# Two layers of graph attention: layer 1's sums in two PSUM banks, its denominators by a matmul of their own, and the second tile's first blocks at the layer change

## The chip, the cores and the metric

The kernel runs on one core of a Trainium2 chip. The metric is the device time of one execution in microseconds (us). The engines are TensorE (PE, with its weight loads as PEld), VectorE (DVE), ScalarE (ACT), GpSimd (POOL), which here mainly issues gathers, and SyncE (SP), which issues the plain DMAs.

## The reference, cut to what matters

There are 3327 nodes with 1024 features, and an adjacency matrix in which about 17 entries of a row are set. Two layers follow each other; each is a graph attention, added to its input and layer-normed.

```python
def layer1(x, adj, W, a1, a2):                      # layer 0 is alike, with 8 heads of 128
    h = x @ W
    e = leaky_relu(h @ a1 + (h @ a2).T, 0.2)
    attention = softmax(where(adj > 0, e, -9e15), axis=1)
    return relu(attention @ h)

x = layernorm(x + layer0(x, adj, ...))
x = layernorm(x + layer1(x, adj, ...))
```

## The kernel before, in words

Nodes are taken in 26 tiles of 128 rows (`NT`). The first part of the kernel makes layer 0's `h` and, for every tile of target rows, lists of the sources that its rows need. The second part, `sparse`, uses these lists. It runs a list of 52 items in order: 26 of class `Layer0` and 26 of class `Target` (layer 1). The prediction calls the latter T0 to T25.

An item works in five blocks of sources, b0 to b4. (Some tiles of layer 0 have two of these done earlier.) For b0 to b3, POOL issues four indirect gathers (`gather`, L1032) of 128 rows each into one of five buffers (`NS`; the profile shows two as `near` and three as `src`). Block b4 (`EB`) is one gather into one of two buffers `end`. The gathers go out in the order of the list `fetches`; `send` issues the next one when a buffer is free and, for layer 1, when the rows of `y_d` that it may read are stored. For b0 and b1 the first half of the tiles must be stored, for b2 to b4 all of them. Five of the early blocks of T0, T1 and T2 stand ahead in that list (`ahead_of`).

In layer 1 a block then takes two steps. In `weights`, DVE makes a 128x128 tile of weights in three operations: two write into columns 256 to 383 of `way`, a PSUM tile of one bank (L1222, L1223), the third writes `es` in SBUF (L1225). In `sums`, PE multiplies these by the gathered rows (L1234). A row of `y_d` holds 1024 values, a one for the denominator, and two factors of the weights. The 1025 columns are cut in three (`CUTS`), one PSUM bank each. In b0 to b3 the four groups of 32 targets use 32 columns of PE each.

When a tile's five blocks are summed, `close` adds the tile's own node, divides, and writes `z` (ACT and DVE). `finish` is a generator of ten steps: two sets of four transposes of `z`, then the projection by layer 1's `W` (`wt1`, L1266) in eight pairs of k-tiles, which PE does between the sums of the next tiles. After each half, DVE adds the residual (L1269). `settle` makes the layer norm and stores the rows.

`pipeline` writes the order of work out by hand. Every engine takes its instructions in that program order. For block j of item i it issues the `weights` of the next block, then the `sums` of this one, then `send` and `rest`, which runs the `finish` steps of the items before by the tables in `plans`. `prepare` of the next item, which loads its row of factors (`rr`), makes its marks (L1048, L1052) and loads its tile of `y_d`, is issued in the middle of an item's blocks. `own` makes a tile's own weight from that tile of `y_d`.

The layer change is at the last `Layer0` item. Its `finish` makes the norm (Sqrt on ACT) and two dot products on DVE, takes two Exp on ACT, and stores the tile's row into `y_d` (L1166). In `pipeline`, `turn` marks T0: four of these steps come ahead of its first weights.

PSUM has eight banks: six of tag A for sums and projections, one for transposes, one for `way`.

Of the kernel before, what the change touches and what calls it, by code (L numbers as in the profile page):

```python
# [19 lines left out]
P = 128  # L20
# [6 lines left out]
def kernel(  # L27
# [50 lines left out]
    HW0 = DW + 2 * H  # L78
    HW = D + 4
    HP = 1088  # L80
# [891 lines left out]
    def sparse(own):  # L972
# [9 lines left out]

        ys = [pool.tile([P, HW], F32, bufs=1, name=f"y{n}") for n in range(3)]
        for y in ys:
            nc.vector.memset(y[:, D:], 0.0)
            nc.vector.memset(y[:, D : D + 1], 1.0)

# [67 lines left out]
        class Layer0:  # L1055
# [86 lines left out]
            def finish(self):  # L1142

                ri = sbuf("ri", [P, H], 2)
                for n, acc in enumerate(self.acc):
                    nc.vector.reciprocal(ri[:, HEADS[n] : HEADS[n + 1]], acc[:, :, DH])
                t, row = self.t, self.y
                y = row[:, :D]
                for h in range(H):
                    yh = y[:, h * DH : (h + 1) * DH]  # L1150
                    nc.vector.scalar_tensor_tensor(  # L1151
                        yh, self.acc[h // 3][:, h % 3, :DH], ri[:, h : h + 1], yh, op0=OP.mult, op1=OP.add
                    )
                yield
                yield from ph.norm_steps([y])
                for n in range(2):
                    pr = sbuf("pr", [P, D], 1)
                    nc.vector.scalar_tensor_tensor(
                        pr, y, 1.0, wa[n], op0=OP.mult, op1=OP.mult, accum_out=r1.sd[:, t, n, :]
                    )  # L1160
                    if n == 0:
                        yield
                nc.scalar.activation(row[:, D + 1 : D + 2], r1.d[:, t, :], AF.Exp)
                nc.scalar.activation(row[:, D + 2 : D + 3], r1.d[:, t, :], AF.Exp, scale=SLOPE)
                nc.scalar.activation(grow[:, t : t + 1], r1.s[:, t, :], AF.Exp, scale=1 - SLOPE)
                nc.sync.dma_start(y_d[t * P : (t + 1) * P, :HW], row)  # L1166
                stored.add(t)
                yield
                tr = bank("T", [P, 4, P], "tr")
                nc.tensor.transpose(tr[:, 0, :], grow[:, t : t + 1].to_broadcast([P, P]), ident)  # L1170
                line = sbuf("line", [1, P], 2)
                nc.scalar.activation(line, tr[:1, 0, :], AF.Copy)
                nc.sync.dma_start(row_d[t], line)

        class Target:
# [3 lines left out]
            def __init__(self, t, n):  # L1179
                self.t, self.n, self.src, self.made, self.buf = t, n, {}, {}, {}  # L1180

# [15 lines left out]
            def own(self):  # L1197

                t, res = self.t, self.res
                es = self.es = sbuf("es1", [P, 2], 2)  # L1200
                nc.vector.scalar_tensor_tensor(
                    es[:, 1:], res[:, D + 1 : D + 2], grow[:, t : t + 1], res[:, D + 2 : D + 3], op0=OP.mult, op1=OP.max
                )
                nc.vector.tensor_tensor(es[:, :1], es[:, 1:], loop[:, t : t + 1], OP.mult)
# [7 lines left out]
            def begin(self):  # L1212
                self.acc = {c: bank("A", [P, CUTS[1]], "acc1") for c in (2, 0, 1)}

            def weights(self, b):
# [5 lines left out]
                oh = self.oh[:, b * NG : (b + 1) * NG, :] if b < EB else self.oh2.unsqueeze(1)  # L1221
                nc.vector.tensor_tensor(raw, r, s[:, :, D + 1 : D + 2].to_broadcast(wide), OP.mult)  # L1222
                nc.vector.tensor_tensor(raw, raw, s[:, :, D + 2 : D + 3].to_broadcast(wide), OP.max)  # L1223
                es = sbuf("es", [P, P], 3).rearrange("p (g t) -> p g t", g=ng)
                nc.vector.tensor_tensor(es, raw, oh, OP.mult)  # L1225
                self.made[b] = es

            def sums(self, b):
                es, s = self.made.pop(b), self.src.pop(b)
                for c in (2, 0, 1):  # L1230
                    m = CUTS[c + 1] - CUTS[c]
                    for g in range(NG if b < EB else 1):
                        to = slice(g * GT, (g + 1) * GT) if b < EB else slice(0, P)
                        nc.tensor.matmul(  # L1234
                            self.acc[c][to, :m], es[:, g, :], s[:, g, CUTS[c] : CUTS[c + 1]],
                            start=b == 0, stop=b == EB,
                        )

            def close(self):

                ri = sbuf("ri", [P, H], 2)
                nc.vector.tensor_tensor(ri[:, 2:3], self.acc[2][:, D - CUTS[2] : D - CUTS[2] + 1], self.es[:, :1], OP.add)
                nc.vector.reciprocal(ri[:, :1], ri[:, 2:3])
                nc.vector.tensor_tensor(ri[:, 1:2], ri[:, :1], self.es[:, :1], OP.mult)  # L1244
                z = self.z = sbuf("z", [P, D], 3)
                for c in (2, 0, 1):
                    cut = slice(CUTS[c], min(CUTS[c + 1], D))
                    nc.scalar.activation(z[:, cut], self.res[:, cut], AF.Copy, scale=ri[:, 1:2])  # L1248
                for c in (2, 0, 1):
                    cut = slice(CUTS[c], min(CUTS[c + 1], D))  # L1250
                    nc.vector.scalar_tensor_tensor(
                        z[:, cut], self.acc[c][:, : cut.stop - cut.start], ri[:, :1], z[:, cut],
                        op0=OP.mult, op1=OP.add,
                    )
# [43 lines left out]
        def pipeline(items, fetches):  # L1298
# [4 lines left out]
                len(Target.blocks) - HB: ((), (2, 1), (1, 1), (1,)),  # L1303
                Target: ((2,), (2, 1), (2, 1), (1, 1), (1, 1), (1,)),
            }

            def rest(i, n):
                it = items[i] if i < len(items) else items[-1]
                plan = plans[Target] if isinstance(it, Target) else plans[len(it.blocks)]
                for who in plan[n]:  # L1310
# [4 lines left out]
            def send():  # L1315
                while sent[0] < len(fetches):
# [3 lines left out]
                    items[i].fetch(b)  # L1320
                    sent[0] += 1

            def get(i):
# [11 lines left out]
            for i, it in enumerate(items):  # L1335
# [4 lines left out]
                for j, b in enumerate(it.blocks):  # L1340
# [8 lines left out]
                    if j == 0:  # L1349
                        get(i + 1)  # L1350
                    if j == nb // 2 and after:
                        after.prepare()
                    if j == 0:
                        it.own()
                    if j + 1 < nb:
                        it.weights(it.blocks[j + 1])
                    elif after and type(after) is type(it):
                        after.weights(after.blocks[0])
                    if j == 0:
                        it.scale_own()  # L1360
                    it.sums(b)
                    free[b == EB].append(it.buf.pop(b))
                    send()
# [18 lines left out]
        fetches = [(i, b) for i, it in enumerate(items[:NT]) for b in it.blocks][HB:]  # L1382
        ahead_of = [(NT + i, b) for i in range(3) for b in range(HB)][: NS]
        fetches += ahead_of
# [161 lines left out]
```

## Time and profile before

| | us |
|---|---|
| median of 3 runs | 1749.48 (1748.37 to 1754.7) |
| the profiled execution | 1751.44 |
| its span, first to last instruction | 1749.6 |
| up to the last layer 0 sums | 1069.8 |
| layer change, until PE runs on without a gap | about 50 |
| layer 1 in steady order, until T25's sums | 598.8 |
| the rest: T24's and T25's projection, last norm, store | 30.8 |

| engine | busy us of the span | share |
|---|---|---|
| PE | 1497.3 | 86% |
| DVE | 1143.2 | 65% |
| POOL | 1050.7 | 60% |
| ACT | 494.6 | 28% |

Each row of a profile's timeline has the start in us, the busy time in us, the engine, the source line (L1234), the operation, what it writes and reads by the program's names, shape and count. In brackets follow the engine's idle time just before it, and what ended that. PE's rows give modelled ends, so rates are read from start to start. PEclk or "granted clock" is TensorE's clock as a share of its full speed.

### The profile page before, as it was taken

The page shows a single profiled execution, that of the slowest core. Times are in us where ns is not written, and L with a number is a line of the kernel's source. Part 1 is how long each engine was busy: PE and PEld are TensorE (multiplying, and loading weights), DVE is VectorE, ACT ScalarE, POOL GpSimd, SP SyncE. Part 2 cuts the span into 40 slices and gives each one's busy share as a digit, 9 for nine tenths or more (in the row PEclk, how much of TensorE's full clock was granted, in tenths as well). Part 3 has the DMA queues.
Part 4 walks back from the last instruction along what each step waited for, and adds up shares of the span by engine and source line. Part 5 has one row for each costly group of instructions (what it writes and reads, how often), then busy time and mean ns, then how long its engine had stood idle before and what let it go on. Part 6 is the DMA issues. An engine that isn't in the chain of part 4 may idle for free.

```text
span 1749.6 us, 34204 instructions
## 1 busy us (share of the span) xinstructions
PE 1497.3 (86%) x12755; PEld 865.2 (49%) x12755; DVE 1143.2 (65%) x3126; ACT 494.6 (28%) x1424; POOL 1050.7 (60%) x1309
## 2 busy tenths in 40 slices
PE   9799989898998477676676664799999999999998
PEld 5566655565665355555555542344444444444443
DVE  6799998888886788676877765344444453444443
ACT  5677752232323133332332322011111011111110
POOL 5433155776775666555656666677667766676750
PEclk9999999999999699887888886899999999999999
DMA  7688988999999999999999999999999999999980
GB/s 186 123 157 164 185 232 305 316 388 348 360 346 355 371 410 412 398 396 384 396 396 386 390 384 383 359 401 393 396 399 386 394 392 387 388 394 410 386 336 36
DMA packets 190321, 596.13 MB, mean 341 GB/s; under 512 B 37914, under 2 KB 47924, under 8 KB 190146
## 3 DMA queue, kind: packets, MB, share of 16 engines
q0 software_dynamic: 131056, 459.23, 73.4%
q1 hardware_dynamic: 58932, 134.36, 20.5%
q8 instruction: 103, 1.69, 0.4%
q14 instruction: 72, 0.59, 0.1%
q10 hardware_dynamic: 158, 0.26, 0.0%
HBM read 593.70 MB, written 54.99 MB: 371 GB/s over the span
## 4 chain that ended last, share of the span: by engine, by line
PE 41%; DMA 17%; DVE 5%; issue 2%; POOL 1%; ACT 0%; DVEq 0%; SPq 0%; ACTq 0%; POOLq 0%
PE mm L1266 22%; PE acc L1234 13%; DMA src<-h_d,idx 7%; DMA own<-h_d 4%; PE acc L1134 3%; DMA near<-h_d,idx 2%; PE acc L1121 2%; DMA src<-y_d,idx 2%; DVE e L1108 2%; PE tr L203 1%; DVE pr L998 1%; DVE y L1151 1%; DMA end<-h_d,idx 1%; DMA av<-in_L_gnn_a_dram 1%; DMA half<-half_d 0%
## 5 line engine op out<-in xcount | busy, mean ns | idle before, releaser
L571 PE MATMUL mm<-wt,xT 128*128 128x384 f32 (+1 forms) x1248 | 415.3, 478 | 0.4 <-DMA xT<-in_x_t_dram 0.4
L1266 PE MATMUL mm<-wt,xT 128*128 128x512 f32 x832 | 387.6, 604 | 0.0
L1032 POOL DMA_INDIRECT src<-y_d,idx x248 | 251.4, 1014 | 122.6 <-PE acc L1234 48.2
L571 PEld LDWEIGHTS mm<-wt,xT 128*128 128x128 f32 x1248 | 230.7, 195 | 130.2 <-issue 36.0
L1266 PEld LDWEIGHTS mm<-wt,xT 128*128 128x128 f32 x832 | 149.7, 189 | 198.9 <-issue 194.0
L1269 DVE SCALAR_TENSOR_TENSOR o<-mm,y 128x512 f32<-128x512 f32 x52 | 35.9, 691 | 317.3 <-PE mm L1266 317.3
L1032 POOL DMA_INDIRECT src<-h_d,idx x152 | 160.2, 1054 | 108.3 <-PE acc L1134 24.8
L1032 POOL DMA_INDIRECT near<-y_d,idx x168 | 171.1, 1018 | 65.7 <-issue 21.7
L1134 PE MATMUL acc<-src,e 128*32 128x129 f32 x2432 | 103.4, 340 | 74.6 <-DVE e L1108 74.6
L691 POOL DMA_INDIRECT near<-h_d,idx x112 | 124.1, 1108 | 51.5 <-issue 23.9
L1032 POOL DMA_INDIRECT near<-h_d,idx x96 | 103.3, 1076 | 75.5 <-DMA src<-h_d,idx 28.6
L1234 PE MATMUL acc<-src,es 128*32 128x341 f32 x1488 | 124.8, 470 | 26.0 <-DVE es L1225 26.0
L1134 PEld LDWEIGHTS acc<-src,e 128*32 128x32 f32 x2432 | 86.8, 138 | 92.6 <-DVE e L1108 81.2
L1248 ACT ACTIVATE z<-y,ri 128x342 f32<-128x342 f32 (+1 forms) x78 | 39.5, 569 | 299.1 <-DVE ri L1244 299.1
L1134 PE MATMUL acc<-near,e 128*32 128x129 f32 x1664 | 68.8, 332 | 58.6 <-DVE e L1108 44.2
L1108 DVE TENSOR_TENSOR e<-oh,way 128x1024 f32<-128x1024 f32 x90 | 109.9, 1221 | 7.9 <-PE acc L1134 0.6
L206 ACT ACTIVATE xT<-tr 128x512 f32<-128x512 f32 x52 | 31.0, 597 | 236.0 <-PE tr L203 236.0
L1134 PEld LDWEIGHTS acc<-near,e 128*32 128x32 f32 x1664 | 57.8, 134 | 70.7 <-DVE e L1108 48.6
L1234 PEld LDWEIGHTS acc<-src,es 128*32 128x32 f32 x1488 | 43.1, 112 | 96.3 <-issue 43.9
L1121 PE MATMUL acc<-own,ident 128*128 128x387 f32 (+1 forms) x156 | 72.0, 547 | 16.7 <-ACT own L1090 16.7
L411 ACT ACTIVATE junk<-ad 128x1664 uint8<-128x1664 uint8 x52 | 83.0, 1595 | 7.6 <-POOL ad L400 6.1
L1234 PE MATMUL acc<-near,es 128*32 128x342 f32 (+1 forms) x1008 | 82.0, 458 | 1.5 <-DVE es L1225 1.5
(225 smaller groups left out, 2378.7 us busy)
## 6 DMA issues: line engine op xcount, KB each, us to landing
own<-h_d SPq DMA_DIRECT2D x26, 524.0 KB
y_d<-y SPq DMA_DIRECT2D x26, 514.0 KB
y<-y_d SPq DMA_DIRECT2D x26, 514.0 KB
xT<-in_x_t_dram SPq DMA_DIRECT2D x26, 512.0 KB
h_d<-ht SPq DMA_DIRECT2D x25, 524.0 KB
y<-in_x_dram SPq DMA_DIRECT2D x25, 512.0 KB
out_dram<-o SPq DMA_DIRECT2D x25, 512.0 KB
ad<-in_adj_dram POOLq DMA_DIRECT2D x25, 415.9 KB
```

The costliest lines, as they stand in the source:

```text
L206: nc.scalar.activation(part, tr, AF.Copy)
L411: nc.scalar.activation(junk, ad[:, n * THR : (n + 1) * THR], AF.Copy, accum_out=self.d[:, n : n + 1])
L571: nc.tensor.matmul(accs[t, c], xT[t][:, k, :], wt[:, k, CUTS0[c] : CUTS0[c + 1]], start=k == 0, stop=k == KT - 1)
L691: nc.gpsimd.indirect_dma_start(out=src[n % 3][:, g, :], out_offset=None, in_=h0_d[:THR, :], in_offset=bass.IndirectOffsetOnAxis(ap=idx[:, ...
L1032: nc.gpsimd.indirect_dma_start(out=s[:, g, :w], out_offset=None, in_=table[:n, :], in_offset=bass.IndirectOffsetOnAxis(ap=idx[:, t, b * NG ...
L1108: nc.vector.tensor_tensor(e, oh.unsqueeze(2).to_broadcast([P, ng, H, wide]), wp.unsqueeze(3).to_broadcast([P, ng, H, wide]), OP.mult,)
L1121: nc.tensor.matmul(self.acc[n].rearrange("p h d -> p (h d)"), ident, part, start=False, stop=False)
L1134: nc.tensor.matmul(self.acc[h // 3][g * GT : (g + 1) * GT, h % 3, :], e[:, g, h, :], rowsof[:, g, h, :], start=j == 0 and h in HEADS, stop ...
L1234: nc.tensor.matmul(self.acc[c][to, :m], es[:, g, :], s[:, g, CUTS[c] : CUTS[c + 1]], start=b == 0, stop=b == EB,)
L1248: nc.scalar.activation(z[:, cut], self.res[:, cut], AF.Copy, scale=ri[:, 1:2])
L1266: nc.tensor.matmul(acc, xT[:, k, :], wt1[:, k, half], start=k == 0, stop=k == KT - 1)
L1269: nc.vector.scalar_tensor_tensor(o[:, half], acc, 0.0, res[:, half], op0=OP.max, op1=OP.add)
```

## The change

It has four parts.

1. A row of `y_d` loses the one for the denominator (and an unused column): 1026 columns for 1028. Layer 1's sums go to two banks of 512 columns.
2. DVE adds up the tile's five weight tiles (`total`, four additions of 128x128). After the end block, PE multiplies `total` by a column of ones. The result is the denominator; it goes to column 384 or 385 of `way`. `close` reads it from there and works in halves.
3. At the layer change, after T0's b0 and b1, the new function `sums_ahead` prepares T1, makes its own weight, and issues the weights and sums of its b0 and b1; T1 has three blocks left then, with a plan of its own (`HB`). All six early blocks of T0 to T2 stand ahead in `fetches`, where there were five.
4. Ahead of the last `Layer0` tile's finish, ACT takes a Sqrt of ones that nothing uses (`warm`).

```diff
-    HW = D + 4
+    HW = D + 2
...
-        for y in ys:
-            nc.vector.memset(y[:, D:], 0.0)
-            nc.vector.memset(y[:, D : D + 1], 1.0)
+        ones = pool.tile([P, 1], F32, bufs=1, name="ones")
+        nc.vector.memset(ones, 1.0)
+        warm = pool.tile([P, 1], F32, bufs=1, name="warm")
...
             def finish(self):            # class Layer0
+                if self.n == NT - 1:
+                    nc.scalar.activation(warm, ones, AF.Sqrt)
...
             def own(self):               # class Target
                 t, res = self.t, self.res
+                if self.begun:
+                    return
...
             def begin(self):
-                self.acc = {c: bank("A", [P, CUTS[1]], "acc1") for c in (2, 0, 1)}
+                if not self.begun:
+                    self.acc = [bank("A", [P, HALF], "acc1") for _ in range(2)]
+                    self.total = sbuf("total", [P, P], 2)
...
             def weights(self, b):
...
                 nc.vector.tensor_tensor(es, raw, oh, OP.mult)
                 self.made[b] = es
+                if b == 0:
+                    self.first = flat
+                else:
+                    nc.vector.tensor_tensor(self.total, self.first if b == 1 else self.total, flat, OP.add)
...
             def sums(self, b):
                 es, s = self.made.pop(b), self.src.pop(b)
-                for c in (2, 0, 1):
-                    m = CUTS[c + 1] - CUTS[c]
+                for c, acc in enumerate(self.acc):
                     for g in range(NG if b < EB else 1):
                         to = slice(g * GT, (g + 1) * GT) if b < EB else slice(0, P)
                         nc.tensor.matmul(
-                            self.acc[c][to, :m], es[:, g, :], s[:, g, CUTS[c] : CUTS[c + 1]],
-                            start=b == 0, stop=b == EB,
+                            acc[to, :], es[:, g, :], s[:, g, c * HALF : (c + 1) * HALF], start=b == 0, stop=b == EB
                         )
+                if b == EB:
+                    k = 3 * P + self.n % 2
+                    self.den = way[:, k : k + 1]
+                    nc.tensor.matmul(self.den, self.total, ones, start=True, stop=True)
...
             def close(self):
-                nc.vector.tensor_tensor(ri[:, 2:3], self.acc[2][:, D - CUTS[2] : D - CUTS[2] + 1], self.es[:, :1], OP.add)
+                nc.vector.tensor_tensor(ri[:, 2:3], self.den, self.es[:, :1], OP.add)
...
                 Target: ((2,), (2, 1), (2, 1), (1, 1), (1, 1), (1,)),
+                HB: ((), (1, 1), (1, 1, 1), (1, 1)),
...
+            def sums_ahead(it):
+                it.prepare()
+                it.begin()
+                it.own()
+                it.begun, it.blocks = True, Target.blocks[HB:]
+                for b in range(HB):
+                    it.weights(b)
+                for b in range(HB):
+                    it.sums(b)
+                    free[False].append(it.buf.pop(b))
+                send()
...
-                    if j == nb // 2 and after:
+                    if j == nb // 2 and after and not turn:
                         after.prepare()
                     if j == 0:
                         it.own()
+                    if turn and j == 1:
+                        it.sums(b)
+                        free[False].append(it.buf.pop(b))
+                        sums_ahead(after)
...
-                    it.sums(b)
-                    free[b == EB].append(it.buf.pop(b))
+                    if b in it.buf:
+                        it.sums(b)
+                        free[b == EB].append(it.buf.pop(b))
...
-        ahead_of = [(NT + i, b) for i in range(3) for b in range(HB)][: NS]
+        ahead_of = [(NT + i, b) for i in range(3) for b in range(HB)]
```

More of the change, by code (lines that the diff above doesn't have):

```diff
@@ L1162, in finish @@
                         yield
-                nc.scalar.activation(row[:, D + 1 : D + 2], r1.d[:, t, :], AF.Exp)
-                nc.scalar.activation(row[:, D + 2 : D + 3], r1.d[:, t, :], AF.Exp, scale=SLOPE)
+                nc.scalar.activation(row[:, D : D + 1], r1.d[:, t, :], AF.Exp)
+                nc.scalar.activation(row[:, D + 1 :], r1.d[:, t, :], AF.Exp, scale=SLOPE)
                 nc.scalar.activation(grow[:, t : t + 1], r1.s[:, t, :], AF.Exp, scale=1 - SLOPE)
@@ L1179, in __init__ @@
             def __init__(self, t, n):
-                self.t, self.n, self.src, self.made, self.buf = t, n, {}, {}, {}
+                self.t, self.n, self.src, self.made, self.buf, self.begun = t, n, {}, {}, {}, False
             def ready(self, b):
@@ L1199, in own @@
                 t, res = self.t, self.res
+                if self.begun:
+                    return
                 es = self.es = sbuf("es1", [P, 2], 2)
                 nc.vector.scalar_tensor_tensor(
[L1202 removed]
+                    es[:, 1:], res[:, D : D + 1], grow[:, t : t + 1], res[:, D + 1 :], op0=OP.mult, op1=OP.max
                 )
@@ L1221, in weights @@
                 oh = self.oh[:, b * NG : (b + 1) * NG, :] if b < EB else self.oh2.unsqueeze(1)
-                nc.vector.tensor_tensor(raw, r, s[:, :, D + 1 : D + 2].to_broadcast(wide), OP.mult)
-                nc.vector.tensor_tensor(raw, raw, s[:, :, D + 2 : D + 3].to_broadcast(wide), OP.max)
-                es = sbuf("es", [P, P], 3).rearrange("p (g t) -> p g t", g=ng)
+                nc.vector.tensor_tensor(raw, r, s[:, :, D : D + 1].to_broadcast(wide), OP.mult)
+                nc.vector.tensor_tensor(raw, raw, s[:, :, D + 1 : HW].to_broadcast(wide), OP.max)
+                flat = sbuf("es", [P, P], 3)
+                es = flat.rearrange("p (g t) -> p g t", g=ng)
                 nc.vector.tensor_tensor(es, raw, oh, OP.mult)
                 self.made[b] = es
+                if b == 0:
+                    self.first = flat
+                else:
+                    nc.vector.tensor_tensor(self.total, self.first if b == 1 else self.total, flat, OP.add)
             def sums(self, b):
                 es, s = self.made.pop(b), self.src.pop(b)
-                for c in (2, 0, 1):
-                    m = CUTS[c + 1] - CUTS[c]
+                for c, acc in enumerate(self.acc):
                     for g in range(NG if b < EB else 1):
@@ L1245, in close @@
                 z = self.z = sbuf("z", [P, D], 3)
[L1246 to L1250, printed above, removed]
+                halves = [slice(c * HALF, (c + 1) * HALF) for c in range(2)]
+                for half in halves:
+                    nc.scalar.activation(z[:, half], self.res[:, half], AF.Copy, scale=ri[:, 1:2])
+                for half, acc in zip(halves, self.acc):
                     nc.vector.scalar_tensor_tensor(
-                        z[:, cut], self.acc[c][:, : cut.stop - cut.start], ri[:, :1], z[:, cut],
-                        op0=OP.mult, op1=OP.add,
+                        z[:, half], acc, ri[:, :1], z[:, half], op0=OP.mult, op1=OP.add
                     )
@@ L1308, in rest @@
                 it = items[i] if i < len(items) else items[-1]
-                plan = plans[Target] if isinstance(it, Target) else plans[len(it.blocks)]
+                plan = plans[len(it.blocks)]
+                if isinstance(it, Target):
+                    plan = plans[Target if it.blocks is Target.blocks else HB]
                 for who in plan[n]:
```

## The prediction

> **What bounds the kernel now.** I read the table of stretches first (busy time of each engine by stretch of the span), then the order of work in the stretch that is longest, then the rows around the layer change. T0, T1, ... are layer 1's target tiles, b0 to b4 their blocks of sources.
>
> ```profile
> 1000.00:1069.80 69.80, 43.63 (x716) 33.47 (x716) 46.03 (x119) 17.69 (x48) 43.74 (x42) 0.80 1.01 383
> 1069.80:1120.00 50.20, 22.74 (x185) 7.97 (x183) 18.47 (x57) 6.29 (x13) 31.39 (x31) 0.69 0.92 356
> 1120.00:1718.80 598.80, 598.80 (x3452) 258.33 (x3449) 265.25 (x796) 71.29 (x145) 405.06 (x400) 1.00 0.98 382
> ```
>
> Columns: length, then busy us of PE, PEld, DVE, ACT, POOL, then granted clock, DMA share, GB/s. From 1120 to 1718.8 us PE is never idle and at full clock, while DVE works 44% of the time and POOL 68%. So whatever a tile of layer 1 costs on PE is paid in full. The 50 us before it, the layer change, have PE busy for 22.7 us at 0.69 of the clock.
>
> A layer 1 tile on PE, from the timeline of PE:
>
> ```profile
> 1399.38 1.89 PE L1234 MATMUL acc<-end,es 128*128 128x341 f32 x6
> ...
> 1418.55 1.93 PE L1234 MATMUL acc<-src,es 128*32 128x341 f32 x24
> 1420.42 3.70 PE L1266 MATMUL mm<-wt,xT 128*128 128x512 f32 x8
> 1423.95 1.89 PE L1234 MATMUL acc<-end,es 128*128 128x341 f32 x6
> 1425.68 3.60 PE L1266 MATMUL mm<-wt,xT 128*128 128x512 f32 x8
> ```
>
> The end block returns after 1423.95 - 1399.38 = 24.57 us, and does so for all later tiles. Each f32 matmul is two instructions. From start to start, a 512-column instruction of the projection takes 429 ns (0.838 ns per column), one of the 342-column sums 287 ns (0.839). In a four-group block the four groups of 32 columns run side by side, so x24 is six sets of 287 ns plus 0.14 us around them: 1.86 us. The price is columns, not instructions.
>
> The layer change, from its timeline:
>
> ```profile
> 1073.93 1.28 ACT L227 ACT_TABLE_LOAD   x1 [4.66 <-DVE sg L226]
> 1079.95 3.65 PE L1234 MATMUL acc<-src,es 128*32 128x341 f32 x24 [10.03 <-DVE es L1225]
> 1086.68 1.00 POOL L1032 DMA_INDIRECT src<-y_d,idx  x1 [4.17 <-PE acc L1234]
> 1099.34 3.62 PE L1234 MATMUL acc<-src,es 128*32 128x341 f32 x24 [12.61 <-DVE es L1225]
> 1103.22 1.00 POOL L1032 DMA_INDIRECT src<-y_d,idx  x1 [5.14 <-PE acc L1234]
> 1104.44 1.93 PE L1234 MATMUL acc<-near,es 128*32 128x341 f32 x24 [1.48 <-DVE es L1225]
> 1116.61 3.52 PE L1234 MATMUL acc<-src,es 128*32 128x341 f32 x24 [2.94 <-DVE es L1225]
> ```
>
> In order: T0 b0 waits 10 us for the last layer 0 row (its chain holds a 1.28 us table load). T0 b2 can be gathered only when that row is stored, from 1086.68, and PE waits 12.6 us for it. T1 b2's gather starts at 1103.22, when T0 b2's buffer is free, and T1 b2 is the last thing PE waits for, until 1116.61.
>
> **The change part by part.** Sums are set against this execution's span of 1749.6 us; it took 1751.44 us, 2.0 us over the median of 1749.48, and the difference is carried over to the median.
>
> *Two banks of 512.* 1025 columns become 1024, six sets per block become four: 6 x 287 = 1722 ns against 4 x 429 = 1716 ns. The 0.14 us around a block, where PE changes between full and 32-column weights, stays. Five blocks save about 0.03 us, 0.04 with a few ns at set borders; 26 tiles, -1.0 us. Narrower gathers (4104 for 4112 bytes) save 0.2% of DMA time that PE does not wait for. No stall is removed: PE had none here.
>
> *The denominator's matmul.* It adds two instructions of one column after the end block, each with 128x128 weights of its own. The nearest row:
>
> ```profile
> 1067.76 1.86 PEld L1126 LDWEIGHTS acc<-end,e 128*128 128x128 f32 x16 [2.10 <-DVE e L1108]
> ```
>
> Sixteen such loads take 1.86 us, 0.11 us apart. There each load starts with the matmul before it. So the first can load under the last 429 ns sum, the second only once the first matmul has started, and the next projection's load after that. So two loads show: 0.22 us. The floor is nothing (all hidden), the ceiling two unhidden loads with their matmuls at 0.21 us, the spacing at the start of that row, plus the wait below: 0.53.
>
> *The wait that it brings.* The sum lands in `way`, column 384 on, the PSUM tile in whose columns 256 to 383 DVE makes the weights. In program order the next tile's b0 weights come ahead of it:
>
> ```profile
> 1424.15 0.69 DVE L1269 SCALAR_TENSOR_TENSOR o<-mm,y 128x512 f32<-128x512 f32 x1 [5.66 <-PE mm L1266]
> 1424.76 0.29 DVE L1222 TENSOR_TENSOR way<-rr,src 128x128 f32<-128x128 f32 x1
> 1425.09 0.30 DVE L1223 TENSOR_TENSOR way<-way,src 128x128 f32<-128x128 f32 x1
> 1425.42 0.29 DVE L1225 TENSOR_TENSOR es<-way,oh 128x128 f32<-128x128 f32 x1
> ```
>
> Does PE have to wait for them, though the columns differ? Layer 0's lists show the like:
>
> ```profile
> 108.08 0.20 ACT L344 ACTIVATE places<-xp 128x2 f32<-128x2 f32 x1
> ...
> 108.32 0.33 PE L491 MATMUL xp<-mvg,place 128*128 128x168 bf16 x3 [0.37 <-ACT places L344]
> ```
>
> L344 reads two columns of `xp`, L491 writes others, and PE waits for ACT. The Trainium skill speaks against this placement too (PSUM — Partial Sum Buffer, "PSUM bank collisions raise a hardware error"): two engines must be kept apart by bank and 32-partition quadrant, not by address. By columns alone the cost is 0.22 us per tile. By bank, the matmul waits for the read that ends at 1425.71, plus 0.06 us for the signal, where four sums from 1423.95 would have let it start at 1425.67: 0.10 more, 0.32. I take the second: 26 x 0.32 = +8.3 us. The first would be +5.7.
>
> *DVE.* Four additions per tile at 0.29 us (L1225's shape) are 1.2 us, against 0.3 saved by two z pieces at 0.69 for three at 0.56. Cover: DVE is idle for half of a tile, waiting for PE; b3's weights, the tightest, are ready 1.8 us before PE needs them, and the additions for b1 and b2 fall long before that. Without cover they would cost 0.9 us per tile. The closing chain now waits for the denominator, some 0.5 us later; behind it on DVE stand the z pieces and b1's weights, which PE needs over 3 us later. ACT's z in halves, the memsets and `ones` are hidden likewise.
>
> *The layer change.* Five moves, walked on the trace of before.
> 1. The early Sqrt loads the table before it is needed: -1.28 us on T0 b0 (1078.7) and on the last row's store.
> 2. T2 b1 is now gathered before T0 b2. It takes T0 b0's buffer at about 1082.5: four gathers at 1.30 us, until 1087.7. The gap before 1086.68 was 4.17 us, so T0 b2 starts about 1.0 us late and its data stands at about 1097.
> 3. T1's preparation comes early: on SP its row and its y tile (issued at 1084.61 and 1085.05 before, now 1.3 us earlier), on DVE two marks of 0.68 and 0.28 us, T1's own weight, which waits for y, and then both blocks' weights. The y load's semaphore was complete at 1092.46, so now about 1091. T0 b2's weights are queued behind all that on DVE, but their data comes later.
> 4. T1 b0 and b1 then run on PE from 1092.6, at half clock first (3.65 and 2.8 us, as T0's did): until about 1099. T0 b2 follows at full clock. PE waits less here, but T0 b3's gather, at 1091.88 before, now needs T1 b0's buffer: about 1096.5. It lands at about 1105 for 1103.4, behind it the end block (1106.7), T1 b2 (gather from 1103.1, the place it had before; data at about 1112.5) and T1 b3 (gather from 1108.3, data at about 1119).
> 5. T0's transposes, in PE's gaps at 1110 and 1113 before, now follow T1 b2: +1.1 us. PE takes T1 b2 at 1113.5, T1 b3 at about 1120, six projection pairs (5.2 us), the end block and two more pairs. It reaches the seventh pair of T0 at about 1132 to 1133; before it was 1132.5.
>
> The clock belongs to this. The Trainium skill (TensorE: Matmul & The Clock Gate, "What's actually happening") has PE go to half rate after an idle window of about 3.4 us; here it was at half after 2.94 us (row 1116.61) and not after 1.48 (row 1104.44). By the page the new shorter gaps stay warm and save 1.7 us; by the rows a gap near 3 us may not. I take -0.7 us for the whole layer change. Its ends: all 12.6 us filled and the data in time, -12; T0 b3 later than I think, +4.
>
> **The sum.** -1.0 + 8.3 - 0.7 = +6.6 us: 1749.5 + 6.6 = about 1756 us, +0.4%. A measurement of this kernel tells about 0.5%, 8.7 us, from no change.
>
> **The rivals.** *A: the denominator's loads stand open.* Place: the end block of every tile. If both loads and matmuls take the 0.21 us seen at the start of L1126, each tile costs 0.53 us: +13.8 - 1.0 - 0.7 = 1761.6 us. It decides from 0.40 us per tile (26 x 0.40 - 1.7 = 8.7). For it: PE cannot load under a matmul of one column. Against: the later loads of that row are 0.11 apart. 30%.
>
> *B: the layer change pays in full.* PE has T1's blocks to do during the 12.6 us, and data for T0 b3 comes without delay: -12, and the denominator hidden, so 1749.5 - 12 - 1.0 = 1736.5 us. With the denominator at 0.22, 1742. For it: 27 us of idle PE in that stretch. Against: T1's two blocks already sat in gaps, and what PE waited for last was data. 12%.
>
> *C: no wait for the bank.* +5.7 - 1.0 - 0.7: 1753.5 us. For it: the columns are disjoint. Against: L491. It is within 0.5%, and so part of the 58% that I give to no change.
>
> The range 1745 to 1764 takes in C with a layer change that gives 8 us, and A with one that loses 2. Faster by over 0.5%: 0.12; within: 0.56; slower: 0.32.
>
> **What would show it.** Right: the end block returns after about 24.85 us for 24.57, the denominator's matmul sits 0.1 us behind DVE's L1225 step of the next tile, and PE's steady run begins within 2 us of where it did. Wrong: a period at or under 24.6 (the matmul is hidden), or over 25.0 (A), PE waiting inside the steady run, or T1 b3's sums before 1116 (B).

## The result and the profile after

The changed kernel takes 1765.42 us (median of 5 runs, 1764.55 to 1769.88). The kernel before, run beside it, takes 1748.37 us. The ratio is 1.0087, with a 95% interval of 1.0065 to 1.0110: 11 to 19 us slower. The forecast was 1756.0. The direction is right, the size is less than half of what came, and the median stands 1.4 us beyond the end of the range (1764).

The page of after: the profiled execution took 1764.55 us, its span is 1762.8 us, 13.2 more than before. The table of stretches (length, busy us of PE, PEld, DVE, ACT, POOL, granted clock, DMA share, GB/s) has the same form as before:

```profile
1068.00:1120.00 52.00, 26.54 (x140) 7.42 (x140) 20.99 (x64) 6.10 (x15) 35.65 (x36) 0.70 0.99 381
1120.00:1740.00 620.00, 617.82 (x2700) 232.09 (x2701) 294.29 (x878) 69.22 (x126) 396.75 (x397) 1.00 0.95 366
```

PE is still full and at full clock in layer 1, on fewer instructions, and the stretch is longer. The lines have moved: the sums are now L1244, the denominator's matmul L1250, the projection L1277, DVE's weights L1228, L1229 and L1232, the addition L1237. One tile on PE's timeline, from end block to end block:

```profile
1407.35 1.88 PE L1244 MATMUL acc<-end,es 128*128 128x512 f32 x4
1409.16 0.38 PE L1250 MATMUL way<-ones,total 128*128 128x1 f32 x2
1409.41 3.68 PE L1277 MATMUL mm<-wt,xT 128*128 128x512 f32 x8
1413.02 1.92 PE L1244 MATMUL acc<-near,es 128*32 128x512 f32 x16
...
1432.30 1.88 PE L1244 MATMUL acc<-end,es 128*128 128x512 f32 x4
```

The period is 1432.30 - 1407.35 = 24.95 us; before it was 24.57. So each tile costs 0.38 more.

To see what belongs to the layer change, I count from the start of layer 0's last matmul in each trace (1069.54 before, 1069.64 after). T2's end block, the first that lies in the steady order, comes at 84.1 us before and at 88.2 after; T25's comes at 649.3 and 662.1. So of 12.8 us up to T25, 4.0 are there at T2, and 8.8 are 23 periods at 0.38. Ahead of T2's end block stand two denominators, T0's and T1's (0.8), so the layer change itself lost about 3.3 us. Its rows in the trace of after, in order of time:

```profile
1079.02 3.64 PE L1244 MATMUL acc<-src,es 128*32 128x512 f32 x16 [9.00 <-DVE es L1232]
1082.91 1.00 POOL L1032 DMA_INDIRECT src<-y_d,idx  x1 [0.85 <-PE acc L1244]
...
1088.12 1.00 POOL L1032 DMA_INDIRECT near<-y_d,idx  x1 [0.31 <-DMA src<-y_d,idx]
...
1092.42 0.22 DVE L1205 SCALAR_TENSOR_TENSOR es<-y,grow 128x1 f32<-128x1 f32 x1 [11.03 <-DMA y<-y_d]
1093.91 3.64 PE L1244 MATMUL acc<-near,es 128*32 128x512 f32 x16 [8.15 <-DVE es L1232]
1097.80 1.00 POOL L1032 DMA_INDIRECT near<-y_d,idx  x1 [3.94 <-PE acc L1244]
1102.34 0.30 DVE L1228 TENSOR_TENSOR way<-rr,near 128x128 f32<-128x128 f32 x1 [7.09 <-DMA near<-y_d,idx]
1103.43 3.64 PE L1244 MATMUL acc<-near,es 128*32 128x512 f32 x16 [3.67 <-DVE es L1232]
...
1122.83 3.32 PE L1244 MATMUL acc<-near,es 128*32 128x512 f32 x16 [2.12 <-DVE es L1232]
```

Read them as a chain of buffers. T0 b0's buffer comes free at 1082.9, and the next gather in the list is T2 b1's, a block that PE sums 60 us later (1142.73). T0 b2's gathers start behind it, at 1088.12. PE fills the time with T1's b0, but not before 1093.91, since T1's own weight heads DVE's queue and waits for T1's tile of `y_d` (11.03 us idle, until 1092.42). Only when these sums are done is there a buffer for T0 b3, whose gather goes out at 1097.80 after POOL has stood idle for 3.94 us. T0 b2's data stands at 1102.34; it was at 1098.33 before. T1 b3, the last block that PE waits for, is summed from 1122.83.

### The profile page after: what moved, and what is told of

Read it like the earlier page. It is cut to its first block, busy times and chain, and to the rows that moved or that the text cites. A ratio compares the mean times of both kernels' runs of the same rounds, so it can differ in the third digit from the quotient of the medians.

```text
span 1762.8 us, 32493 instructions
## 1 busy us (share of the span) xinstructions
PE 1505.1 (85%) x11923; PEld 829.4 (47%) x11923; DVE 1170.5 (66%) x3199; ACT 489.6 (28%) x1399; POOL 1042.5 (59%) x1309
## 4 chain that ended last, share of the span: by engine, by line
PE 42%; DMA 15%; DVE 7%; issue 2%; ACT 0%; POOL 0%; DVEq 0%; SPq 0%; ACTq 0%; POOLq 0%
PE mm L1277 21%; PE acc L1244 13%; DMA src<-h_d,idx 5%; PE acc L1134 3%; DMA own<-h_d 3%; DMA near<-h_d,idx 2%; PE acc L1121 2%; DVE e L1108 2%; DMA src<-y_d,idx 2%; PE tr L203 1%; DMA half<-half_d 1%; DMA near<-y_d,idx 1%; DVE y L1153 1%; DVE pr L998 1%; DVE st L224 1%
## 5 line engine op out<-in xcount | busy, mean ns | idle before, releaser
L1277 PE MATMUL mm<-wt,xT 128*128 128x512 f32 x832 | 389.5, 607 | 0.0
L1032 POOL DMA_INDIRECT src<-y_d,idx x244 | 244.9, 1003 | 127.0 <-issue 39.0
L571 PEld LDWEIGHTS mm<-wt,xT 128*128 128x128 f32 x1248 | 230.1, 194 | 129.4 <-issue 34.4
L1277 PEld LDWEIGHTS mm<-wt,xT 128*128 128x128 f32 x832 | 148.2, 190 | 221.4 <-issue 221.4
L1244 PE MATMUL acc<-src,es 128*32 128x512 f32 x976 | 119.6, 608 | 9.0 <-DVE es L1232 9.0
L1261 ACT ACTIVATE z<-y,ri 128x512 f32<-128x512 f32 x52 | 34.7, 714 | 321.3 <-DVE ri L1257 321.3
L1244 PE MATMUL acc<-near,es 128*32 128x512 f32 x688 | 90.0, 644 | 15.7 <-DVE es L1232 15.7
L1090 ACT ACTIVATE own<-own,es 128x129 f32<-128x129 f32 x208 | 63.8, 390 | 60.6 <-DVE es L1083 43.1
```

What stands on the lines that cost most here:

```text
L571: nc.tensor.matmul(accs[t, c], xT[t][:, k, :], wt[:, k, CUTS0[c] : CUTS0[c + 1]], start=k == 0, stop=k == KT - 1)
L1032: nc.gpsimd.indirect_dma_start(out=s[:, g, :w], out_offset=None, in_=table[:n, :], in_offset=bass.IndirectOffsetOnAxis(ap=idx[:, t, b * NG ...
L1090: nc.scalar.activation(h[:, d], h[:, d], AF.Copy, scale=self.es[:, n : n + 1])
L1244: nc.tensor.matmul(acc[to, :], es[:, g, :], s[:, g, c * HALF : (c + 1) * HALF], start=b == 0, stop=b == EB)
L1261: nc.scalar.activation(z[:, half], self.res[:, half], AF.Copy, scale=ri[:, 1:2])
L1277: nc.tensor.matmul(acc, xT[:, k, :], wt1[:, k, half], start=k == 0, stop=k == KT - 1)
```

## The experiments

In each, the layer change is judged by T2's end block, counted as above, the steady order by the period, and the whole by the ratio to the kernel before.

| kernel | T2's end block | period | T25's end block | ratio (95%) |
|---|---|---|---|---|
| before | 84.1 | 24.57 | 649.3 | |
| after | 88.2 | 24.95 | 662.1 | 1.0087 (1.0065 to 1.0110) |
| e1_no_den | 87.6 | 24.53 | 651.8 | 1.0030 (1.0016 to 1.0044) |
| e2_den_bank | 87.6 | 24.75 | 656.9 | 1.0064 (1.0044 to 1.0084) |
| e3_no_turn | 81.3 | 24.95 | 655.2 | 1.0053 (1.0034 to 1.0073) |
| e4_warm | 83.9 | 24.57 | 649.1 | 0.9999 (0.9982 to 1.0016) |
| e5_five_ahead | 81.2 | 24.95 | 655.1 | 1.0043 (1.0020 to 1.0065) |
| e6_turn_alone | 90.9 | 24.57 | 656.0 | 1.0047 (1.0032 to 1.0061) |
| e7_early | 84.4 | 24.57 | 649.5 | 1.0003 (0.9990 to 1.0015) |
| e8_adds | 84.1 | 24.57 | 649.3 | 0.9998 (0.9986 to 1.0010) |
| e9_three_banks_five | 82.9 | 24.57 | 648.1 | 1.0004 (0.9992 to 1.0016) |
| e10_two_banks_best | 81.1 | 24.75 | 650.4 | 1.0018 (1.0008 to 1.0027) |

The end blocks are counted in one trace of each kernel, the ratio over all its executions. In the changed kernel, e1 to e3, e5, e6, e9 and e10 the ratio stands 1.5 to 3.6 us above what T25's end block gives. Most of that lies within the intervals, and no run here explains it.

Two more, e11_wide_rows and e12_no_turn_again, fell on a chip on which every kernel was slower, and are told at their place.

My theory after the result: the denominator's matmul is what the longer period is made of, and the order at the layer change costs the rest through the buffers. The rivals: that two banks are dearer than three, that DVE's additions hold PE up, that the early Sqrt or the order gains and something else loses more.

### The denominator: e1_no_den and e2_den_bank

e1 is the changed kernel without the matmul, so it divides by one and the own weight, and not by the denominator:

```diff
-                    nc.tensor.matmul(self.den, self.total, ones, start=True, stop=True)
+                    self.den = ones
```

> The changed kernel without the denominator's matmul: close divides by a constant one plus the own weight, so the division is not the reference's; the additions on VectorE stay. Theory P (the matmul and its two weight loads stand open on TensorE): the end block returns after 24.53 us in place of 24.95, 0.03 to 0.04 under the kernel before, and the run is 10 to 11 us shorter than the changed kernel, about 3 to 5 us over the kernel before, which is the layer change. Rival V (the additions on VectorE or the 512-column blocks cost the time): the period stays at 24.9 us.

The period is 24.53. So two banks of 512 save 0.04 us per tile, and the matmul costs 24.95 - 24.53 = 0.42, all of the difference and a little more. T2's end block stays at 87.6: the layer change isn't the matmul's doing.

e2 is the changed kernel with the sum in the bank of the transposes, which DVE's weights don't use:

```diff
-                    k = 3 * P + self.n % 2
-                    self.den = way[:, k : k + 1]
+                    self.den = bank("T", [P, 4, P], "den")[:, 0, :1]
```

> The changed kernel with the denominator in a tile of the transposes' bank, where VectorE makes no weights. If the wait for VectorE's weights at the end block is a wait for the bank, it goes: the denominator's matmul follows 1.72 us after the end block's start, not 1.81, the period falls from 24.95 to 24.86 us, and the run is about 2.3 us shorter than the changed kernel. Rival (the matmul waits for its own weights or for the array): the period stays 24.95.

The period is 24.75: the wait for the bank of `way` costs 0.20 us, not the 0.10 that I had given it. The weight loads (PEld) show why. First the changed kernel, at the tile shown above, with the step of DVE that it waits for:

```profile
1408.21 0.19 PEld L1244 LDWEIGHTS acc<-end,es 128*128 128x128 f32 x1 [0.24 <-issue]
1409.16 0.30 PEld L1250 LDWEIGHTS way<-ones,total 128*128 128x128 f32 x2 [0.76 <-DVE es L1232]
1409.38 0.30 PEld L1277 LDWEIGHTS mm<-wt,xT 128*128 128x128 f32 x2
```

```profile
1408.82 0.29 DVE L1232 TENSOR_TENSOR es<-way,oh 128x128 f32<-128x128 f32 x1
1409.58 0.16 DVE L1255 TENSOR_TENSOR ri<-way,es 128x1 f32<-128x1 f32 x1 [0.47 <-PE way L1250]
```

Then e2, the same place in a tile:

```profile
1407.12 0.19 PEld L1244 LDWEIGHTS acc<-end,es 128*128 128x128 f32 x1 [0.24 <-issue]
1407.54 0.19 PEld L1249 LDWEIGHTS den<-ones,total 128*128 128x128 f32 x1 [0.24 <-PE acc L1244]
1407.97 0.19 PEld L1249 LDWEIGHTS den<-ones,total 128*128 128x128 f32 x1 [0.24 <-issue]
1408.08 0.30 PEld L1276 LDWEIGHTS mm<-wt,xT 128*128 128x128 f32 x2
```

In e2 the first of the two loads starts at 1407.54, under the end block's last sum, and the matmul follows that sum at once. In the changed kernel it isn't the matmul that waits but its weight load: it is put down to `DVE es L1232`, which ends at 1409.11, and it starts at 1409.16. So the wait costs its own 0.10 us and also uncovers the load that would have been hidden, another 0.11. Without the wait, the matmul costs 24.75 - 24.53 = 0.22 us.

### The layer change: e3_no_turn and e4_warm

e3 is the changed kernel with the old order at the layer change and five early blocks; banks, denominator and the early Sqrt stay:

```diff
-        ahead_of = [(NT + i, b) for i in range(3) for b in range(HB)]
+        ahead_of = [(NT + i, b) for i in range(3) for b in range(HB)][: NS]
...
-                    if j == nb // 2 and after and not turn:
+                    if j == nb // 2 and after:
...
-                    if turn and j == 1:
+                    if False:
```

> The changed kernel with the old order at the layer change: no early blocks of the second tile, five early gathers; two banks, denominators and the early Sqrt stay. If the layer change lost 3 us beyond the denominators, PE's steady run starts about 3 us sooner than in the changed kernel and the run is 3 us shorter, some 9 to 10 us over the kernel before (period 24.95 us). Rival (the new order gained, and all the loss is the denominators): the run is 1 us or more longer than the changed kernel.

T2's end block comes at 81.3, 6.9 us ahead of the changed kernel. So the new order loses more than the 3.3 us by which the two kernels differ at the layer change, and something else in the change gives some 3.5 back.

e4 is the kernel before with the early Sqrt alone:

```diff
+                if self.n == NT - 1:
+                    nc.scalar.activation(warm, ones, AF.Sqrt)
```

> The kernel before with the early Sqrt alone. Theory: the last row's norm ends 1.3 us sooner (as the first sums did in the changed kernel, at 1079.0 for 1080.0), the last row is stored sooner, and PE's steady run with it: about 1 us faster than before, which these rounds can hardly tell from none; the profile shows it at the first sums of layer 1. Rival: the gathers behind the store are held by the DMA engines, and only the first sums move.

T0 b0 gains what was expected and T2's end block gains nothing to speak of (84.1 to 83.9). The rows of T0 b0 and T0 b2 in e4, where layer 0's last matmul starts at 1074.68:

```profile
1084.02 3.49 PE L1239 MATMUL acc<-src,es 128*32 128x341 f32 x24 [8.95 <-DVE es L1230]
...
1104.42 3.53 PE L1239 MATMUL acc<-src,es 128*32 128x341 f32 x24 [14.79 <-DVE es L1230]
```

T0 b0 is at 9.3 us for 10.4 before, T0 b2 at 29.7 for 29.8. The gain turns into a longer wait for T0 b2's data (14.79 us for 12.61).

e3 and e4 have the same order of work and the same early Sqrt; e3 has two banks and the denominator's matmul. Yet e3 is 2.6 us ahead at T2's end block, with two denominators (0.8) to pay before it: the two-bank kernel is some 3.4 us better at the layer change, which my steps did not have. T0 b2's sums start at 28.4 us after layer 0's last matmul for 29.7 in e4, T1 b2's at 45.4 for 46.9, and T1 b2 then runs at full clock. T1 b2 in e3, then in e4:

```profile
1113.63 1.92 PE L1244 MATMUL acc<-src,es 128*32 128x512 f32 x16 [1.43 <-DVE es L1232]
```

```profile
1121.63 3.46 PE L1239 MATMUL acc<-src,es 128*32 128x341 f32 x24 [2.88 <-DVE es L1230]
```

1.5 us by the earlier start and 1.5 by the clock are 3.0 of the 3.4. T0 b2's gathers start alike (16.2 us after layer 0's last matmul, 16.1 in e4), and its data still is 1.3 us earlier. POOL's last gather before them goes out at 10.9 us in e3 and at 12.2 in e4: one gather less, of 1.30 us, is left to issue when layer 0 ends. Whether that is the two banks' doing is asked again below.

### The order or the sixth gather: e5_five_ahead and e6_turn_alone

e5 is the changed kernel with one line put back: five early blocks, the new order kept.

```diff
-        ahead_of = [(NT + i, b) for i in range(3) for b in range(HB)]
+        ahead_of = [(NT + i, b) for i in range(3) for b in range(HB)][: NS]
```

> The changed kernel with five early gathers in place of six: T2's b1 no longer goes ahead of T0's b2. Theory O (the order of gathers is the loss at the layer change): T0's b2 is gathered when the last row is stored, about 3.6 us sooner than in the changed kernel, and T0's b3 takes the buffer of T0's b1 and waits for no sums; its data comes some 6 us sooner, and T1's b3 too. T2's end block, 88.2 us after the last layer 0 sums in the changed kernel, comes at 81 to 83 us, and the run is about 6 us shorter (period 24.95 us as before). Rival W (the loss is work of T0 moved behind T1's blocks, or T1's late load of y): it stays within 2 us of 88.

e6 is the other side: the kernel before (three banks, denominators from the column of ones, no early Sqrt) with the new order and six early blocks, part 3 of the change alone.

> The kernel before (three banks, a column of ones, no early Sqrt) with the new order at the layer change and six early gathers. Theory: the order loses about 3 us by itself: T2's end block at 87 to 88 us after the last layer 0 sums for 84.2 before, period 24.57 us, the run about 3 us slower than before. Rival (only the two banks make the early blocks slow): within 1 us of before.

One line brings T2's end block from 88.2 to 81.2 us, and part 3 alone takes the kernel before from 84.1 to 90.9, more than the 87 to 88 expected. What loses is the sixth early gather. The other half of the part, T1's blocks ahead on PE, is worth next to nothing: e5 against e3, with the old order, is 81.2 to 81.3. First POOL's row for T0 b2 in e5, then PE's rows for T1 b0, for T1 b1 with T0 b2 right behind it, for T0 b3, and for T1 b3 (layer 0's last matmul starts at 1066.00 in e5, so 3.6 us are to be added for a comparison with the rows of after):

```profile
1082.10 0.99 POOL L1032 DMA_INDIRECT src<-y_d,idx  x1 [5.51 <-DMA y_d<-y]
```

```profile
1088.75 3.33 PE L1244 MATMUL acc<-near,es 128*32 128x512 f32 x16 [8.10 <-DVE es L1232]
1091.91 3.81 PE L1244 MATMUL acc<-src,es 128*32 128x512 f32 x32
1098.81 3.42 PE L1244 MATMUL acc<-near,es 128*32 128x512 f32 x16 [3.09 <-DVE es L1232]
...
1111.94 3.52 PE L1244 MATMUL acc<-src,es 128*32 128x512 f32 x16 [1.99 <-DVE es L1232]
```

T0 b2 has a buffer waiting for it and goes out as soon as the last row is stored, 16.1 us after layer 0's last matmul (18.5 in after). T0 b3 takes T0 b1's buffer and goes out right behind it, where in after POOL stood idle for 3.94 us. T1 b3's sums start at 45.9 us instead of 53.2.

### Is it T1's tile of y_d? e7_early

T1's own weight waits for its tile of `y_d` (1092.42, 11.03 us idle). e7 is the kernel before with the early Sqrt, the new order, five early blocks, and T1's two loads issued ahead of the last norm, where SP isn't yet queued behind the last row's store:

```diff
             def prepare(self):
-                t = self.t
+                self.load()
+                self.oh, self.oh2 = marks(self.t)
+
+            def load(self):
...
                         if turn:
+                            after.load()
                             for _ in range(4):
```

> A version for the layer change: the kernel before (three banks, column of ones) with the early Sqrt, T1's b0 and b1 ahead, five early gathers, and T1's two loads issued before the last layer 0 row's norm, so that T1's sums follow T0's b1 at once. Theory: T0's b2 and b3 are gathered one after the other from the store on, T1's b2 and b3 follow with no wait for a buffer, T2's end block comes 78 to 80 us after the last layer 0 sums for 84.2 before; period 24.57 us; 4 to 6 us faster than before, 0.3%. Rival (the data of b2 to b4 comes no faster than the DMA engines bring it, whatever the order): within 2 us of the kernel before.

The expected gain did not come: T2's end block is at 84.4, the ratio 1.0003. T1 b0 now runs right behind T0 b1, as meant, but DVE, and PE behind it, wait for gathered data instead. DVE's rows for T1 b1 and T0 b2 in e7:

```profile
1090.07 0.30 DVE L1233 TENSOR_TENSOR way<-rr,src 128x128 f32<-128x128 f32 x1 [4.86 <-DMA src<-y_d,idx]
...
1100.22 0.30 DVE L1233 TENSOR_TENSOR way<-rr,src 128x128 f32<-128x128 f32 x1 [9.13 <-DMA src<-y_d,idx]
```

The stretches of 20 us from 1070 to 1130 in e7 have the DMA engines full throughout:

```profile
1070.00:1090.00 20.00, 9.14 (x78) 3.09 (x77) 11.78 (x35) 3.69 (x9) 12.53 (x13) 0.74 1.02 396
1090.00:1110.00 20.00, 9.79 (x73) 3.02 (x74) 3.63 (x12) 0.00 (x0) 15.43 (x16) 0.57 1.02 395
1110.00:1130.00 20.00, 15.72 (x81) 6.93 (x81) 6.20 (x20) 2.72 (x5) 14.71 (x16) 0.91 1.02 398
```

PE is busy for 34.7 of these 60 us, and what it waits for is data. Doing a block of T1 sooner doesn't bring T0 b2's bytes sooner. Against e9 below, which lacks the early loads and nothing else, they come later: T0 b2's weights start 30.1 us after layer 0's last matmul for 28.4, and T2's end block 1.5 us later. As far as e7 shows, the wait for T1's tile of `y_d` matters in the changed kernel only through the buffer that it holds, and not for PE's own time.

### The additions: e8_adds

e8 is the kernel before with DVE's four additions per tile, whose result nothing uses:

```diff
+                if b == 0:
+                    self.first = flat
+                else:
+                    nc.vector.tensor_tensor(self.total, self.first if b == 1 else self.total, flat, OP.add)
```

> The kernel before with the four additions of weight tiles per tile on VectorE, whose sum nothing uses. Theory: hidden in VectorE's waits, the period stays 24.57 us and the time within 0.2%. Rival: they delay weights that TensorE needs, and the period grows by up to 0.9 us.

The period stays at 24.57 us. From 1130 to 1700 us DVE has 278.5 us of work for 257.1 before, and PE is never idle. The additions are hidden.

### The parts put together: e9_three_banks_five and e10_two_banks_best

e9 is the kernel before with the early Sqrt and the new order with five early blocks: e6 with the sixth gather taken out and the Sqrt added. e10 is the changed kernel with the edits of e2 and e5 together.

> The kernel before (three banks, denominator from the ones column) with the early Sqrt and with T1's two first blocks ahead at the layer change, five blocks gathered early. My theory: the order loses only because the sixth early gather takes T0 b0's buffer; with five, T0 b2 to b4 and T1 b2 go out without a gap, so T2's end block comes about 80 us after the last layer 0 sums (84.1 before, 90.9 with six), the period stays 24.57, and the kernel is about 4 us faster than before (ratio 0.998). The rival: the gain seen with five in the two-bank kernel belongs to its shorter closing and bank order, not to the gathers; then 84 to 88 us here and no gain (ratio 1.000 to 1.002).

> The changed kernel with two of its three losses taken away: five blocks gathered early for six, and the denominator's matmul into the bank of the transposes. If the losses add: T2's end block at 80.6 us after the last layer 0 sums (81.2 with five early blocks less 3 x 0.2), a period of 24.75, and T25's end block at about 650 us after the last layer 0 sums (649.3 before, 662.1 in the changed kernel): level with before, ratio 1.000 to 1.001. The rival: the bank of the transposes is held longer when the gathers come earlier, so PE then waits there: a period of 24.85 or more and 652 us or more, ratio 1.003.

e9: taking the sixth gather away is worth 90.9 - 82.9 = 8.0 us here too (0.2 of it the Sqrt's), so that loss doesn't hang on the two banks. But the 80 us that I had expected did not come, nor did a gain in the times (1.0004). I had carried e5's 81.2 over to three banks, and with it what the two-bank kernels have besides; against e4, its like with the old order, the order with five gains 1.0 us here and 0.1 in the two-bank pair. The ratio is the one that the rival gave; T2's end block lies between the two.

e10: the losses add. T2's end block was expected at 80.6 and came at 81.1; the period (24.75) and T25's end block (650.4 for 650) came as expected. The ratio is a little above the 1.001 given. No version tried is faster than the kernel before.

### What two banks give at the layer change: e11_wide_rows and e12_no_turn_again

e11 is e3 with the rows of `y_d` as wide as before; e12 is e3 again.

```diff
-    HW = D + 2
+    HW = D + 4
...
+        for y in ys:
+            nc.vector.memset(y[:, D:], 0.0)
```

> The changed kernel with the old order at the layer change and five early blocks (as e3_no_turn), but rows of y_d of 1028 columns as before instead of 1026, the added ones unused. Open is why e3, with the old order, has T2's end block at 81.3 us where the kernel before with the early Sqrt has 83.9: in e3 T0 b2's sums start 28.4 us after the last layer 0 sums (29.7 before), T1 b2's 1.5 us earlier, and its block runs at full clock (1.92 us for 3.46). If the shorter rows bring the data sooner: T0 b2 at 29.7, T1 b2 cold, T2's end block at 84 to 85. If it is the two banks (the shorter sums, or what layer 0's end leaves in the queues): 28.4 and 81.3 again. Period 24.95 in both cases.

> e3_no_turn run again, for a second profile. If its early layer change belongs to the two banks or the rows: T0 b2's sums at 28.4 us and T2's end block at 81.3, within 0.3. If it was that execution's chance: 29 to 30 us, and 83 to 85. Ratio 1.0053 again, within its interval of 1.0034 to 1.0073.

These do not answer what they were run for. On their chip the kernel before took 1812.55 us, for 1749 to 1751 elsewhere; T0 b2's sums start at 33.0 us in e11 and at 25.8 in e12, T2's end block comes at 93.5 and 93.0, and T0's alone is 7.0 us apart between the two profiles (41.4 and 34.4). The ratios, 1.0037 (1.0011 to 1.0062) and 1.0040 (1.0013 to 1.0067), agree with each other and with e3's 1.0053 within their intervals: four columns more or less in a row make no difference that can be seen, where a difference of 4 us would be hard to see. But e12 is e3's own kernel, and in it POOL's last gather before T0 b2's goes out 3.0 us after layer 0's last matmul, for 10.9 in e3, and T0 b2's sums start 2.6 us sooner. So how much layer 0 leaves in the queue moves T0 b2's data by more than the 1.3 us in question, with the same banks. Whether two banks shorten that queue stays open.

## Why the prediction was right or wrong

**Two banks: right in the steady order.** -0.03 to -0.04 us per tile in the working, -0.04 in e1. At the layer change, where I gave them nothing, the two-bank kernels are better by about 3.4 us (e3 against e4) and 2.5 (e5 against e9), the denominators taken off; that the banks are the cause is not shown.

**The matmul's two loads: right in sum.** 0.22 us per tile, as e2 less e1 measures. Its parts are not quite those named: from the matmul to the projection it is 0.14 us in e2, and the eight projection matmuls behind it take 3.61 us for the 3.53 in e1, as the projection's second load (in the x2 row at 1408.08 above) seems to stand open as well.

**The wait for the bank: real, and twice the size given.** This is the term of the sum that failed for the steady order. I gave 0.10 us, the time from the last sum to the read's end, and left the first load hidden under that sum. The load itself waits, so it is exposed: 0.20 us measured. Over 26 tiles that is 2.6 us. Rival C (no wait for the bank, by columns) is refuted by e2. Rival A put 0.53 us on each tile; 0.42 lies between it and my 0.32, above its point of decision of 0.40, but by another mechanism than A's: without the wait, the loads cost 0.22, not 0.53.

**DVE and the closing chain: hidden, as said.** e8 for the additions; PE does not wait for the later `z` in the steady order.

**The early Sqrt: right and worth nothing.** Its step (-1.28 us on T0 b0) came as 1.1 us in e4, and e4 shows the stall that takes its place: T0 b2's data.

**The layer change: wrong.** Forecast -0.7 us, with +4 as its bad end; it came out at +3.3. By the runs that is +6.9 for the new order (after against e3), about -3.4 by which the two-bank kernel is better, and -0.2 for the Sqrt. That the sum falls inside the ends given is luck: neither the loss nor the gain was in the walk. The step that failed is step 2: it let T2 b1 take T0 b0's buffer and charged T0 b2 1.0 us for it, with its data at 1097. Its gathers were to end at about 1092.6 by the same step, so that left 4.4 us for landing, where the rows of before show 6.8 (issued until 1091.58, weights from 1098.33). They ended at 1093.87, and the data stood at 1102.34, 8.5 us later. Step 4 was right in its chain, T0 b3 waiting for T1 b0's buffer, and 1.3 us early (1096.5 for 1097.80). T1 b3 came at 1122.83 for about 1120 and took 1.4 us longer, at half clock: these 2.8 and 1.4 make up, within 0.2, the 4.0 us between forecast and result. PE's steady run began 4 us later than before, not within the 2 us that I gave as the sign of being right. (The "six projection pairs" in 5.2 us of step 5 are three pairs of k-tiles, and its "seventh pair", at 1132.5 before, is the sixth.) Behind this is a question not asked: I walked the order as one piece and not with five early gathers beside six. The piece holds a loss of 7 to 8 us, the sixth gather (e5, e9), and a gain of 0.1 to 1.0, the rest. Rival B (the layer change pays in full, -12) fails at its own cover: e7 does the work in the wait, and PE then waits for DMA.

**The clock.** The rule of the Trainium skill that I weighed (TensorE: Matmul & The Clock Gate, "What's actually happening") is half rate after an idle window of about 3.4 us. Read as the length of one gap, it would have kept all these shorter gaps warm. T1 b2 did stay warm: it took 3.52 us before and 1.92 after. But T1 b3 then ran at half, 3.32 us for 1.92, behind a gap of 2.12 us, so what the rule promised was gained once and lost once. The length of the gap isn't what decides: in e10 the same block ran at half behind 1.14 us, where in e3 T1 b2 ran at full behind 1.43.

```profile
1116.12 3.57 PE L1244 MATMUL acc<-src,es 128*32 128x512 f32 x16 [1.14 <-DVE es L1232]
```

The same section has the window run freely, whatever the kernel does. That is what the traces show: PE's clock stays at full or at half for a multiple of 3.41 us each time, in after with changes at 1101.81, 1112.05, 1122.29 and 1125.70. What counts is how much PE did in the whole of such a window. The window just before T1 b3 in after, the one before T1 b3 in e10, and the one of the gap before T1 b2 in e3, in the form of the tables of stretches; the clock fell behind the first two and stayed full behind the third:

```profile
1118.88:1122.29 3.41, 1.15 (x8) 0.67 (x7) 0.87 (x3) 1.19 (x2) 2.73 (x3) 1.00 1.01 412
1112.84:1116.25 3.41, 1.58 (x16) 0.97 (x16) 1.06 (x4) 1.19 (x2) 2.62 (x3) 1.00 1.03 413
1111.25:1114.66 3.41, 1.98 (x20) 0.83 (x20) 1.94 (x6) 0.60 (x1) 2.71 (x3) 1.00 1.03 418
```

PE was busy for 1.15 and 1.58 us where the clock fell, and for 1.98 where it did not. Neither of the two windows was idle, so the measurement is against a rule that asks for an idle one. And where a gap lies in these windows is chance to the kernel: the 1.5 us that the clock gave e3 over e4 may be luck too.

**The sum.** 26 x 0.38 = 9.9 us for the steady order (forecast 7.3) and 3.3 for the layer change (forecast -0.7) make 13.2, the difference of the two spans; up to T25's end block, which one denominator follows, it is 12.8. The ratio stands for 15 us, with 13.2 inside its interval (11 to 19). No change was given the most (0.56; the 58% beside rival C is a slip), slower 0.32; it is slower by the bound of 0.5%.

## What to carry to other kernels

A sum that rides along as one more column of matmuls that run anyway is nearly free (here 0.04 us per tile with all that the third bank cost); as a matmul of its own, one column wide, it costs 0.22 us, and 0.42 where it shares a PSUM bank with another engine's work. Where a queue hands out buffers in the order of a list, a block moved ahead delays every block behind it: ask who needs a buffer first, and try the list apart from the order of the work. Before filling an idle engine with work brought forward, look at the DMA share of that stretch: in e7 it rose to 1.02, and the data that PE waited for came no sooner.

## What the runs showed of the hardware

- A matmul's wait for a PSUM bank held its weight load back too, so a wait of 0.10 us cost 0.20 (e2 against the changed kernel), though the columns of the bank were disjoint.
- PE's clock kept to windows of 3.41 us: in all 14 traces every stretch at one clock lasts a multiple of that. Around the layer change it fell only behind windows with PE busy for 1.75 us or less, and rose only behind 2.66 or more (the kernel before, the changed one, e1 to e7, e9 and e10). The gap before a block doesn't decide by its length: half clock after 1.14 us (e10), full after 1.43 (e3).
- A block's data stood 8.5 us after its last gather had left POOL (after, T0 b2), although its 2.1 MB (4 x 128 rows of 4104 bytes) are 5.3 us of the 400 GB/s that e7's stretches show. The DMA engines weren't full all that time: from 1098 to 1102 us their share was 0.77, so a full queue is not the whole reason.
